# A scatter-add of graph messages: more groups sent as pairs, one product for a pair, leftovers of 112 rows, kept groups one at a time

## The chip, the cores and the metric

One core of a Trainium2 chip. The metric is the device time of one execution in microseconds; the kernel before takes 3864.85 us, the median of three runs (3861.75 to 3872.72). A core has engines with instruction streams of their own: TensorE (PE; its weight loads are shown as PEld), VectorE (DVE), ScalarE (ACT), GpSimd (POOL) and SyncE (SP, which here issues transfers). They wait for each other, and for transfers, on semaphores.

## The reference

A graph layer: 12500 nodes with 128 features, 400000 edges with 20 edge features. Edges are sorted by `dst`; `src` is random. Cut to what matters:

```
h   = relu(layernorm(x)) @ W_in2f.T
Wij = (smu(edge_attr @ W_f1.T + b_f1) @ W_f2.T + b_f2) * edge_weight[:, None]
x_ij = h[dst] * Wij                                  # one 128-float message per edge
agg = segment_sum(x_ij, src, num_segments=12500)     # added up by src
out = x + smu(agg @ W_o1.T + b_o1) @ W_o2.T + b_o2
```

Gathering `h[dst]` is easy, since `dst` is sorted and a run of edges touches a window of few nodes. Adding up by `src` is not: the messages must first be brought into the order of `src`.

## The kernel before, in words

**Tiles, groups, epochs.** The edges are cut into 3125 tiles of 128, groups of 4 tiles (`GRP`) and supergroups of 8 (`SUP`, two groups): 391 supergroups, 782 groups. The nodes are cut into 98 bins of 128. The supergroups are cut into ten epochs (`PARTS`); each epoch has a buffer in HBM with `CAP` rows for each bin, and three such buffers are used in turn. `CAP` follows from the mean number of rows in a bin, `SIGMA` deviations and the share of pairs, rounded up to 128 rows.

**Making messages.** In each step of the main loop the engines work on a few neighbouring groups at different stages: PE `hide`, ACT `bend` (the gelu), PE `gather` (one-hot times the window of h), ACT `take` (scaled by the weight, L945), PE `weigh` (L970, L972), DVE `mix` (the product, L1002), which writes the message tile `ms`: four tiles of 128 features and, in column 128, the node's place within its bin. There are nine message tiles; one is free again when its scatter has landed.

**Where a row goes.** DVE marks each edge's bin (`bins`), PE counts ranks within bins (`count`, L735), DVE reads them (`read`, L779) and makes row numbers `ix` (`number`). POOL then scatters the message rows into the epoch's buffer, one indirect transfer of 128 rows for each tile (L1072).

**Pairs.** In a paired group tiles 0 and 1 are matched with tiles 2 and 3: an edge of the first half is put beside an edge of the second half that has the same bin and rank, and both go as one row of double width. The keys of the first half are spread over a PSUM bank by PE (`spread_keys`, L813), DVE compares them (`match`, L822, which counts the matches in `met`), PE ranks the unmatched rows (`rank_left`, L832) and DVE makes a permutation of them (`place_left`, L839, L840). A step later PE permutes the second half by 12 passes (`permute`, L859), ACT takes the result out of PSUM (`take_pairs`, L870, L871), and POOL sends two transfers of 128 double rows. The unmatched rows, the leftover `lt`, are sent with a later group, its host, which also counts them (`el`, L707). A pair takes two scatters and one for its leftover, a plain group four. In the kernel before, the product of a pair is made in two halves: tiles 0 and 1 into `ms` (L992), tiles 2 and 3 into a tile `cd` of two buffers (L991), with a copy of the places for each (L995 or L997). From epoch 1 on, and after group 80 of epoch 0, about every third group is a pair.

**Kept groups.** The 23 supergroups of the last two epochs are made early, spread over epochs 1 to 4 (the list `flow`), both groups in a row. Their message rows are written to HBM (`kept_rows`), not scattered; at the end, in the late loop, they are fetched again (`refill`) and scattered while the sums of the last epochs run. A kept group passes the PSUM bank `pt` on its way (`turn`, L1027), and ACT copies it out (L1040). Nine of them are paired in the late loop.

**Summing.** While epoch k is scattered, the buffer of epoch k-1 is fetched (`rw`), DVE makes one-hot matrices of the places (`choose`, L1117) and PE adds the rows up into `agg` (L1130, 4116 products in all, of two passes each). The number of products follows from `CAP` alone.

**Order.** PE, DVE, ACT and SP run their instructions in the order in which the code gives them; the main loop writes that order out by hand, step by step. Work that is not tied to a step, such as reading later edge indices (`head_of`), stands in a timetable, with slots that the loop passes three times a step: `fetched` issues the transfers of `dst_col` and `src_col`, and `based` (L410) is DVE's first use of them. `double` (L644) is an ACT copy of the bins that DVE's `mark_bins` (L654) reads.

**The guard.** If a bin overflows, or a pair matches too few rows, a flag is set and the kernel computes everything again in a slow, general way.

Of the kernel before, what the change touches and what calls it, by code (L numbers as in the profile page):

```python
# [20 lines left out]
P = 128  # L21
# [11 lines left out]
PARTS = (60, 58, 58, 58, 47, 37, 27, 23, 16, 7)  # L33
EVERY = (4, 3, 3, 3, 3, 3, 3, 3)
UNPAIRED = 10
MOST_PAIRS = 224
FIRST_PAIRED = 80
LATE_EVERY = 3
# [3 lines left out]
SIGMA = 4.95  # L42
# [8 lines left out]
def gnn_kernel(  # L51
# [46 lines left out]
    for a, n in eps_of:  # L98
        last_groups = UNPAIRED / (SUP // GRP)
        paired = n - last_groups if 0 < len(CAP) < len(eps_of) - 1 else 0  # L100
        if not CAP:
            paired = max(0, n - last_groups - FIRST_PAIRED / (SUP // GRP))
        every = LATE_EVERY if len(CAP) >= len(eps_of) - SENT_LAST else EVERY[len(CAP)]
        mean = (n + WIDER * paired / every) * SUP * P * P / N
        dev = SIGMA * math.sqrt((n + 2 * WIDER * paired / every) * SUP * P * P / N)
        CAP.append(math.ceil((mean + dev) / P) * P)
        ZMIN.append(max(0, math.floor((n * SUP * P * P / N - dev) / ZP) * ZP) if len(ZMIN) < BUFS else 0)
# [14 lines left out]
    SPILLS = 2  # L122
# [222 lines left out]
    with tc.tile_pool(name="ld", bufs=4) as ld, \  # L345
# [121 lines left out]
        met = const.tile([P, 2 * MOST_PAIRS], F16, name="met")  # L467
        h_first = met.bitcast(BF)[:, :3 * D].rearrange("p (b k d) -> p b k d", b=1, k=3)
# [57 lines left out]
        seq = [s * PER + i for s in flow for i in range(PER) if s * PER + i < NG]  # L526

# [11 lines left out]
        for p, g in enumerate(seq):  # L539
# [3 lines left out]
            if wanting and p >= wanting[0][0] + 5:  # L543
                host[g] = wanting.pop(0)[1]
                assert epoch[g // PER] == epoch[host[g] // PER]
            elif (since_pair >= (math.floor, math.ceil)[len(paired) % 2](EVERY[epoch[g // PER]])
                  and (epoch[g // PER] or p >= FIRST_PAIRED) and seq[p - 1] // PER < EARLY and g + UNPAIRED < ends_of[epoch[g // PER]]):
                paired[g] = len(paired)
                wanting.append((p, g))
                since_pair = 0  # L550
        assert not wanting
        LATE_END = eps_of[-1][0] * PER - 1
        late_pairs = list(range(EARLY * PER + LATE_EVERY - 1, LATE_END - 3, LATE_EVERY))
        pair_no = {g: i for i, g in enumerate(list(paired) + late_pairs)}
        assert 2 * len(pair_no) <= met.shape[1]
        late_keys = const.tile([P, len(late_pairs), GRP], F32, name="late_keys")
# [91 lines left out]
        def mark_bins(s):  # L648
# [3 lines left out]
            es = cnt.tile([P, SUP // 2, NB], F16, name="es", bufs=1)  # L652
# [129 lines left out]
        def number(g):  # L782
# [4 lines left out]
            if s_of(g) < EARLY:  # L787
                ix = cnt.tile([P, GRP + 1], I32, name="ix", bufs=12)
# [18 lines left out]
        keys_of, left_of, matched, apart_of = {}, {}, {}, {}  # L807

        def spread_keys(g):

            kt = ps1.tile([P, GRP * P], F32, name="pt")
# [4 lines left out]
        def match(g):  # L816
# [3 lines left out]
            o = 2 * pair_no[g]  # L820
            for i in range(2):
# [3 lines left out]
                                               op0=ALU.is_equal, op1=ALU.mult, accum_out=met[:, o + i:o + i + 1])  # L825
            matched[g] = (kt, pp)

        def rank_left(g):

            kt, i = matched[g][0], 2 * pair_no[g]  # L830
            at_ = kt[:, 2 * P:2 * P + 2]
            nc.tensor.matmul(at_, tri, met[:, i:i + 2], start=True, stop=False, skip_group_check=True)  # L832
            nc.tensor.matmul(at_[:, 1:2], ones_h, met[:, i:i + 1], start=False, stop=True, skip_group_check=True)
# [17 lines left out]
        def permute(g):  # L851

            pp, cd = matched.pop(g)[1], apart_of.pop(g)
            po = ps1.tile([P, GRP * P], F32, name="pt")
            for j in range(3):
                w = ROW + 1 if j == 2 else ROW
                for i in range(2):
                    o = (4 + i if j == 2 else 2 * i + j) * P
                    nc.tensor.matmul(po[:, j * (ROW + 1):j * (ROW + 1) + w], pp[:, o:o + P], cd[:, i, :w],  # L859
                                     start=(i == 0), stop=(i == 1))  # L860
            matched[g] = po

        def take_pairs(g):

            po, ms, k = matched.pop(g), mixed[g], epoch[s_of(g)]
            lt = cnt.tile([P, ROW + 1], F32, name="lt", bufs=3)
# [3 lines left out]
            nc.scalar.activation(ms[:, 1::2, :], po[:, :o].rearrange("p (j r) -> p j r", j=2)[:, :, 0:ROW], AF.Copy)  # L870
# [105 lines left out]

        def mix(g):
# [3 lines left out]
            if by_edge(g):  # L981
                t, n = groups[g]
                ms = msg.tile([P, GRP, ROW], F32, name="ms")
                pw, hg = pws.pop(g), rows_of.pop(g)
                if g in paired:
                    k = epoch[s_of(g)]
                    m, t0, hic = k // BUFS, *begins[k]
                    cd = msg.tile([P, 2, ROW + 1], F32, name="cd", bufs=2)
                    pw, hg = [v.rearrange("p (j f) -> p j f", f=P) for v in (pw, hg)]
                    nc.scalar.activation(taken[g][:, :2], keys_of[g][:, :2], AF.Copy)  # L990
                    nc.vector.tensor_tensor(cd[:, :, 0:P], pw[:, 2:], hg[:, 2:], op=ALU.mult)  # L991
                    nc.vector.tensor_tensor(ms[:, 0::2, 0:P], pw[:, :2], hg[:, :2], op=ALU.mult)  # L992
                    for to, a in ((cd, t + 2), (ms[:, 0::2], t)):
                        if m:
                            nc.scalar.activation(to[:, :, P], lo_b[:, a:a + 2], AF.Identity, bias=mark[:, m:m + 1])  # L995
                        else:
                            nc.scalar.activation(to[:, :, P], lo_b[:, a:a + 2], AF.Copy)  # L997
                    nc.scalar.activation(cd[:, :, P + 1], hic[:, t + 2 - t0:t + 4 - t0], AF.Identity, bias=shift)
                    apart_of[g] = cd
                    mixed[g] = ms  # L1000
                    return
                nc.vector.tensor_tensor(ms[:, :n, 0:P], pw.rearrange("p (j f) -> p j f", f=P)[:, :n],  # L1002
# [27 lines left out]
        def send(g):  # L1030
# [5 lines left out]
            ms = msg.tile([P, GRP, ROW], F32, name="ms")  # L1036
# [17 lines left out]
        def scatter(g, ms):  # L1054

            ix = taken.pop(g)
            if g in pair_no:
                for j in range(2):
                    scatter_rows(g, ms[:, 2 * j:2 * j + 2].rearrange("p j r -> p (j r)"), ix[:, j:j + 1])
# [3 lines left out]
            if g in host:  # L1063
                scatter_rows(g, left_of.pop(host[g])[0], ix[:, GRP:])
# [168 lines left out]
        ms = msg.tile([P, GRP, ROW], F32, name="ms")  # L1233
# [205 lines left out]
        for c in range(1, NC):  # L1439
# [3 lines left out]
            due(t + 0.5 - (SOONER if t < known else 0), stages.pop(0))  # L1443
# [193 lines left out]
        for p in range(len(seq)):  # L1637
# [80 lines left out]
            if p % PER == 0:  # L1718
                double(sup_at(p // PER + 2), nc.scalar)
# [39 lines left out]
        def refill(g):  # L1759
            if g < NG:  # L1760
                t, n = groups[g]
                back[g] = msg.tile([P, GRP, ROW], F32, name="ms")
                if g in pair_no:
                    t0, hic = begins[epoch[s_of(g)]]
                    cd = apart_of[g] = msg.tile([P, 2, ROW + 1], F32, name="cd", bufs=2)
                    nc.sync.dma_start(back[g][:, 0::2, :], kept_rows[:, t - kept_tile:t - kept_tile + 2, :])
                    nc.sync.dma_start(cd[:, :, 0:ROW], kept_rows[:, t - kept_tile + 2:t - kept_tile + 4, :])
                    nc.scalar.activation(cd[:, :, P + 1], hic[:, t + 2 - t0:t + 4 - t0], AF.Identity, bias=shift)
                    mixed[g] = back[g]
                    return  # L1770
                nc.sync.dma_start(back[g][:, :n, :], kept_rows[:, t - kept_tile:t - kept_tile + n, :])

        def flag_formed():

            few_met = ps1.tile([P, GRP * P], F32, name="pc")[:, :2 * len(pair_no)]
            nc.tensor.matmul(few_met, ones_h, met[:, :2 * len(pair_no)], start=True, stop=True)
            sums = mv.rearrange("p b s -> p (b s)")[:, :len(pair_no)]
            nc.vector.tensor_reduce(sums, few_met.rearrange("p (g i) -> p g i", i=2), op=ALU.add, axis=AX.X)
            least_met = const.tile([P, 1], F32, name="least_met")
            nc.vector.tensor_reduce(least_met, sums, op=ALU.min, axis=AX.X)  # L1780
            i = 4 + 2 * EPOCHS
            nc.vector.tensor_scalar(bad[:, i:i + 1], least_met, float(P), None, op0=ALU.is_lt)
# [27 lines left out]
        def place_of_left(g):  # L1810
# [4 lines left out]
            ix = ranks[g] = cnt.tile([P, GRP + 1], I32, name="ix", bufs=12)  # L1815
# [258 lines left out]
```

## Time and profile before

| | |
|---|---|
| median of three runs | 3864.85 us |
| the profiled execution | 3877.55 us, span 3875.5 us |
| PE / DVE / ACT / POOL busy | 85% / 79% / 73% / 75% |
| indirect transfers on POOL | 2578 + 192 + 163 |
| bytes moved | 904.79 MB, 233 GB/s on average |

How to read it: the page has each engine's busy time, the span in 40 slices, the transfer queues, the chain that ended last, and groups of instructions by line. A row of a group has the line, engine, operation, what it writes and reads, the count, busy us in all and mean ns of one; then the idle time of the engine before these, and what ended it. L12 is line 12 of the kernel. An indirect transfer's length on POOL is the time in which POOL makes its descriptors, not that of its data. An engine's idle time is put down to the event that came last before it went on, which need not be what it waited for.

### The profile page before, as it was taken

What the parts mean: (1) busy time and instruction counts of PE and PEld (TensorE: products, weight loads), DVE (VectorE), ACT (ScalarE), POOL (GpSimd) and SP (SyncE); (2) the same over time, 40 slices, a digit from 0 to 9 for tenths busy, and PEclk for the clock granted to TensorE, in tenths of its full rate; (3) what the DMA queues carried; (4) which work ended last, traced back from release to release, by engine and by line L of the source; (5) the groups of instructions that cost most, each with busy time, mean ns of one, the idle gap of its engine ahead of it and who ended that gap; (6) DMA issues with size and microseconds to landing.
All of it is one profiled execution on the core that took longest, in us unless ns stands there. A gap on an engine that the chain in (4) does not pass through costs nothing.

```text
span 3875.5 us, 89505 instructions
## 1 busy us (share of the span) xinstructions
PE 3289.4 (85%) x27505; PEld 2851.7 (74%) x27505; DVE 3066.3 (79%) x8171; ACT 2831.6 (73%) x8043; POOL 2889.8 (75%) x2977
## 2 busy tenths in 40 slices
PE   8766677888888888899888889899989988999667
PEld 4345555777777777788777778788888878888557
DVE  7887786778777888888888888888888877888557
ACT  7776666778777888788888888788877876776102
POOL 6777777777677777777777777777777777777776
PEclk9988898999999999999999999999999999999889
DMA  5887878889897877788887878878888888887988
GB/s 155 225 238 222 235 222 236 243 242 257 249 264 222 230 220 222 225 238 230 227 225 221 239 213 249 235 230 234 246 234 237 245 233 226 237 237 213 285 258 241
DMA packets 663934, 904.79 MB, mean 233 GB/s; under 512 B 180372, under 2 KB 463128, under 8 KB 663322
## 3 DMA queue, kind: packets, MB, share of 16 engines
q1 hardware_dynamic: 556025, 666.99, 63.4%
q0 software_dynamic: 100112, 219.73, 17.6%
q10 hardware_dynamic: 7312, 12.29, 0.9%
q8 instruction: 223, 3.65, 0.4%
q14 instruction: 262, 2.14, 0.2%
HBM read 500.66 MB, written 398.03 MB: 232 GB/s over the span
## 4 chain that ended last, share of the span: by engine, by line
PE 31%; DVE 17%; DMA 17%; issue 8%; ACT 8%; POOL 7%; SPq 1%; DVEq 0%; ACTq 0%; POOLq 0%
DMA buf<-ms,ix 11%; PE pg L1130 10%; POOL buf L1072 7%; PE pw L970 6%; PE pt L859 5%; PE pc L735 3%; ACT hg L945 3%; DVE se L1117 3%; DVE pc L779 2%; DMA rbc<-rel_dram 2%; DVE mt L822 2%; DVE ms L1002 2%; PE ph L926 2%; DVE eo L654 2%; DMA buf<-lt,ix 2%
## 5 line engine op out<-in xcount | busy, mean ns | idle before, releaser
L1072 POOL DMA_INDIRECT buf<-ms,ix x2578 | 2506.5, 972 | 846.6 <-issue 566.1
L1130 PE MATMUL pg<-se,rw 128*128 128x128 f32 x8036 | 1171.4, 285 | 116.6 <-DVE se L1117 52.7
L1130 PEld LDWEIGHTS pg<-se,rw 128*128 128x128 f32 x8036 | 1042.0, 195 | 162.6 <-DVE agg L1144 56.6
L945 ACT ACTIVATE hg<-ph,w_sb 128x128 f32<-128x128 f32 x2784 | 788.6, 364 | 491.3 <-PE ph L926 468.0
L970 PE MATMUL pw<-w_f,ge 128*128 128x128 f32 x5568 | 778.3, 284 | 12.7 <-DVE ms L1002 7.6
L970 PEld LDWEIGHTS pw<-w_f,ge 128*128 128x128 f32 x5568 | 701.1, 197 | 31.1 <-ACT ge L898 8.0
L1117 DVE TENSOR_TENSOR se<-irow_ps,rw 128x1536 f32<-128x1536 f32 (+1 forms) x345 | 587.4, 1703 | 94.3 <-DMA rw<-buf 74.6
L779 DVE TENSOR_REDUCE pc<-pc 128x4 f32<-128x392 f32 (+1 forms) x782 | 463.6, 593 | 154.5 <-PE pc L735 150.4
L617 ACT ACTIVATE oh<-rbc,nrow 128x512 bf16<-128x512 uint8 x724 | 538.2, 743 | 38.9 <-DMA rbc<-rel_dram 38.9
L618 ACT ACTIVATE oh<-oh,onesb 128x512 bf16<-128x512 bf16 x742 | 535.3, 721 | 24.2
L1002 DVE TENSOR_TENSOR ms<-pw,hg 128x512 f32<-128x512 f32 x513 | 351.4, 685 | 128.5 <-PE pw L972 42.6
L859 PE MATMUL pt<-cd,mt 128*128 128x129 f32 (+1 forms) x2304 | 311.2, 287 | 82.4 <-DVE at L839 76.1
L735 PE MATMUL pc<-eo,tri 128*128 128x392 f16 x782 | 266.9, 341 | 110.2 <-DVE ix L801 88.4
L859 PEld LDWEIGHTS pt<-cd,mt 128*128 128x128 f32 x2304 | 286.5, 199 | 96.5 <-issue 49.6
L926 PE MATMUL ph<-hw,oh 126*128 126x128 bf16 x2784 | 280.7, 224 | 24.0 <-ACT hg L945 24.0
L898 ACT ACTIVATE ge<-pu 128x512 f32<-128x512 f32 x452 | 275.6, 610 | 18.7 <-PE pu L890 16.7
L735 PE MATMUL pc<-so,ones_h 128*128 128x392 f16 (+1 forms) x965 | 281.4, 314 | 0.0
L972 PE MATMUL pw<-wls,f 128*128 128x128 bf16 x2784 | 273.7, 222 | 0.0
L735 PEld LDWEIGHTS <-ones_h 128*128 128x128 f16 x1554 | 154.9, 100 | 149.1 <-issue 32.7
L926 PEld LDWEIGHTS <-oh 126*128 126x128 bf16 x2784 | 220.0, 100 | 45.6 <-issue 28.1
L654 DVE TENSOR_TENSOR eo<-irow_ps,ed 128x784 f16<-128x784 f16 x391 | 218.2, 558 | 37.2 <-ACT ed L644 34.2
L1072 POOL DMA_INDIRECT buf<-lt,ix x192 | 185.9, 968 | 65.5 <-issue 28.7
(339 smaller groups left out, 5088.7 us busy)
## 6 DMA issues: line engine op xcount, KB each, us to landing
rw<-buf SPq DMA_DIRECT2D x292, 774.0 KB
f<-f_parts SPq DMA_DIRECT2D x370, 240.0 KB
buf<-zero SPq DMA_DIRECT2D x146, 387.0 KB
rbc<-rel_dram SPq DMA_DIRECT2D x389, 128.0 KB
buf<-ms,ix POOLq DMA_INDIRECT x2578
f_parts<-hs SPq DMA_DIRECT2D x104, 360.0 KB
rw<-buf SPq DMA_DIRECT2D x49, 645.0 KB
f_parts<-hs SPq DMA_DIRECT2D x106, 240.0 KB
```

The costliest lines, as they stand in the source:

```text
L617: nc.scalar.activation(oh, loaded[s][1][:, o:o + n], AF.Abs, bias=pneg if s < FEW // SUP else nrow)
L618: nc.scalar.activation(oh, oh, AF.Relu, scale=-1.0, bias=onesb[:, 0:1])
L735: nc.tensor.matmul(to, by, of, start=start, stop=stop, skip_group_check=True)
L779: nc.vector.tensor_reduce(sl[:, :n], pc[:, :n], op=ALU.max, axis=AX.X)
L859: nc.tensor.matmul(po[:, j * (ROW + 1):j * (ROW + 1) + w], pp[:, o:o + P], cd[:, i, :w], start=(i == 0), stop=(i == 1))
L926: nc.tensor.matmul(ph[:, j * P:(j + 1) * P], oh[:3 * WIN, a:a + P], hw[:3 * WIN, g % PER, :], start=True, stop=True)
L945: nc.scalar.activation(hg[:, j * P:(j + 1) * P], rows_of[g][:, j * P:(j + 1) * P], AF.Copy, scale=w_sb[:, t + j:t + j + 1])
L970: nc.tensor.matmul(pw[:, a:a + P], ge[:, a:a + P], w_f2, start=(a == 0), stop=False, skip_group_check=True)
L1002: nc.vector.tensor_tensor(ms[:, :n, 0:P], pw.rearrange("p (j f) -> p j f", f=P)[:, :n], hg.rearrange("p (j f) -> p j f", f=P)[:, :n], op=A ...
L1072: i = nc.gpsimd.indirect_dma_start(out=(wide if g in host or g in pair_no else bufs)[k][:, :], out_offset=bass.IndirectOffsetOnAxis(ap=ix, ...
L1117: nc.vector.tensor_tensor(se[:, a:a + n], own.unsqueeze(1).to_broadcast([P, n, P]), rows_in[c][:, a:a + n, P:P + 1].to_broadcast([P, n, P] ...
L1130: nc.tensor.matmul(pgs[0][:, g, :], rows_in[c][:, o, 0:P], sel[c][:, o, :], start=(q == 0), stop=(q == Q[k] - 1))
```

## The change

- `PARTS`: one supergroup goes from epoch 0 to epoch 7. `SIGMA` 4.95 becomes 4.6.
- Pairs: every 3 groups in epoch 0 from group 50 on (before: 4, from 80), and at 2 and 3 groups in turn in epochs 1 to 7 (before: 3). A group is a pair ahead of being a host, and not within two places behind a kept group (before: one).
- A pair's product is one instruction, into a message tile seen as two halves of 2 x 129 + 1 columns; `permute` reads its second half from there, and `take_pairs` writes the permuted rows back over it. `cd` is gone.
- Leftovers are sent with 112 rows, and the guard's bound is raised to 144 matches. A leftover has six tiles (before: three); in the late loop it lies in free tiles of another kind.
- Kept groups alternate with sent ones.
- `double` is called one step earlier for later supergroups; every head's `fetched` is due nine slots earlier, not only the first heads'; `es` has two buffers, `ix` ten (before: twelve).
- Late loop: five groups are fetched ahead (before: four), the keys are spread in the bank `pw`, and `place_of_left` comes ahead of `number_left`.
- Some constants move into space that is free by then (`late_keys` into `mv`, further match counts into `down`).

```diff
-PARTS = (60, 58, 58, 58, 47, 37, 27, 23, 16, 7)
-EVERY = (4, 3, 3, 3, 3, 3, 3, 3)
+PARTS = (59, 58, 58, 58, 47, 37, 27, 24, 16, 7)
+EVERY = (3,) + (2.5,) * 7
-FIRST_PAIRED = 80
-LATE_EVERY = 3
+FIRST_PAIRED = 50
+LATE_OF = 1, 3
+LATE_FREE = 6
+LEFT_ROWS = 112
-SIGMA = 4.95
+SIGMA = 4.6
...
+        for p in reversed(range(len(seq) - 1)):
+            a, b = seq[p:p + 2]
+            if a // PER >= EARLY and a % PER and b // PER < EARLY:
+                seq[p], seq[p + 1] = b, a
...
-            if wanting and p >= wanting[0][0] + 5:
-                host[g] = wanting.pop(0)[1]
-            elif (since_pair >= (math.floor, math.ceil)[len(paired) % 2](EVERY[epoch[g // PER]])
-                  and (epoch[g // PER] or p >= FIRST_PAIRED) and seq[p - 1] // PER < EARLY and g + UNPAIRED < ends_of[epoch[g // PER]]):
+            k = epoch[g // PER]
+            if (since_pair >= (math.floor, math.ceil)[len(paired) % 2](EVERY[k]) and (k or p >= FIRST_PAIRED)
+                    and max(seq[p - 2:p]) // PER < EARLY and g + UNPAIRED < ends_of[k]):
                 paired[g] = len(paired)
                 wanting.append((p, g))
                 since_pair = 0
+            elif wanting and p >= wanting[0][0] + 5:
+                host[g] = wanting.pop(0)[1]
...
-            es = cnt.tile([P, SUP // 2, NB], F16, name="es", bufs=1)
+            es = cnt.tile([P, SUP // 2, NB], F16, name="es", bufs=2)
...
-                ix = cnt.tile([P, GRP + 1], I32, name="ix", bufs=12)
+                ix = cnt.tile([P, GRP + 1], I32, name="ix", bufs=10)
...
-            kt = ps1.tile([P, GRP * P], F32, name="pt")
+            kt = ps1.tile([P, GRP * P], F32, name="pt" if g in paired else "pw")
...
-                    nc.tensor.matmul(po[:, j * (ROW + 1):j * (ROW + 1) + w], pp[:, o:o + P], cd[:, i, :w],
+                    nc.tensor.matmul(po[:, j * (ROW + 1):j * (ROW + 1) + w], pp[:, o:o + P], ms[:, i, ROW:ROW + w],
...
-            lt = cnt.tile([P, ROW + 1], F32, name="lt", bufs=3)
+            lt = cnt.tile([P, ROW + 1], F32, name="lt", bufs=6) if g in paired else late_left(g)
...
-            nc.scalar.activation(ms[:, 1::2, :], po[:, :o].rearrange("p (j r) -> p j r", j=2)[:, :, 0:ROW], AF.Copy)
+            nc.scalar.activation(ms[:, :, ROW:2 * ROW], po[:, :o].rearrange("p (j r) -> p j r", j=2)[:, :, 0:ROW], AF.Copy)
...
-                    nc.vector.tensor_tensor(cd[:, :, 0:P], pw[:, 2:], hg[:, 2:], op=ALU.mult)
-                    nc.vector.tensor_tensor(ms[:, 0::2, 0:P], pw[:, :2], hg[:, :2], op=ALU.mult)
-                    for to, a in ((cd, t + 2), (ms[:, 0::2], t)):
-                        if m:
-                            nc.scalar.activation(to[:, :, P], lo_b[:, a:a + 2], AF.Identity, bias=mark[:, m:m + 1])
-                        else:
-                            nc.scalar.activation(to[:, :, P], lo_b[:, a:a + 2], AF.Copy)
-                    nc.scalar.activation(cd[:, :, P + 1], hic[:, t + 2 - t0:t + 4 - t0], AF.Identity, bias=shift)
+                    nc.vector.tensor_tensor(by_tile(ms)[:, :, :, 0:P], pw, hg, op=ALU.mult)
+                    place = lo_b[:, t:t + GRP].rearrange("p (a u) -> p a u", a=2)
+                    if m:
+                        nc.scalar.activation(by_tile(ms)[:, :, :, P], place, AF.Identity, bias=mark[:, m:m + 1])
+                    else:
+                        nc.scalar.activation(by_tile(ms)[:, :, :, P], place, AF.Copy)
+                    nc.scalar.activation(ms[:, :, 2 * ROW], hic[:, t + 2 - t0:t + 4 - t0], AF.Identity, bias=shift)
...
-                scatter_rows(g, left_of.pop(host[g])[0], ix[:, GRP:])
+                scatter_rows(g, left_of.pop(host[g])[0][:LEFT_ROWS], ix[:LEFT_ROWS, GRP:])
...
-            due(t + 0.5 - (SOONER if t < known else 0), stages.pop(0))
+            due(t + 0.5 - SOONER, stages.pop(0))
...
-            if p % PER == 0:
-                double(sup_at(p // PER + 2), nc.scalar)
+            if p == 0 or p % PER:
+                double(sup_at(-(-p // PER) + 2), nc.scalar)
...
-        for g in range(g1, g1 + 4):
+        AHEAD_OF = 5
+        for g in range(g1, g1 + AHEAD_OF):
             refill(g)
```

The helper that gives the pair's product its view of the tile:

```python
def as_pairs(ms):
    return ms.rearrange("p (u r) -> p u r", u=2)

def by_tile(pairs):
    return pairs[:, :, 0:2 * ROW].rearrange("p u (a r) -> p a u r", a=2)
```

106 lines of the change are left out of this document (63 added, 43 removed).

## The prediction

> **What bounds the kernel now.** I read the page first (busy shares), then GpSimd's own rows, then the span cut into its stages, then the sums of waits.
>
> ```profile
> span 3875.5 us, 89505 instructions
> PE 3289.4 (85%) x27505; PEld 2851.7 (74%) x27505; DVE 3066.3 (79%) x8171; ACT 2831.6 (73%) x8043; POOL 2889.8 (75%) x2977
> ```
>
> By busy time PE is the fullest engine and POOL is one of three at about three quarters. That reading misleads for POOL. Its rows by line, and its own timeline (start, length, idle before it):
>
> ```profile
> L1072 POOL DMA_INDIRECT buf<-ms,ix x2578 | 2506.5, 972 | 846.6 <-issue 566.1 <-DMA buf<-ms,ix 40.5 <-ACT hg L945 27.8
> L1072 POOL DMA_INDIRECT buf<-lt,ix x192 | 185.9, 968 | 65.5 <-issue 28.7 <-DVE ix L804 7.9 <-DVE pc L779 3.7
> L1072 POOL DMA_INDIRECT buf<-ms,ix_kept x163 | 156.7, 962 | 49.7 <-issue 46.0 <-DMA buf<-ms,ix_kept 1.8 <-DMA hic<-in_x 0.3
> ```
>
> ```profile
> 1205.90 0.96 POOL L1072 DMA_INDIRECT buf<-ms,ix  x1 [0.30 <-DMA buf<-ms,ix]
> 1207.16 0.96 POOL L1072 DMA_INDIRECT buf<-ms,ix  x1 [0.30 <-DVE ix L801]
> 1208.43 0.96 POOL L1072 DMA_INDIRECT buf<-ms,ix  x1 [0.30 <-issue]
> ```
>
> Each scatter is preceded by the same 0.30 us, whoever is named as its releaser: the name is chance, the gap is part of the price. So one scatter costs 0.97 + 0.30 = 1.27 us of POOL, and 2578 + 192 + 163 = 2933 of them take 3725 of the 3875 us. The 192 leftovers also count the pairs. By stage (busy of each engine, number of its instructions, granted clock):
>
> ```profile
> core 0: us, PE busy (x) PEld busy (x) DVE busy (x) ACT busy (x) POOL busy (x), PEclk, DMA share, GB/s
> 250.00:700.00 450.00, 312.61 (x2475) 257.05 (x2475) 333.39 (x986) 305.90 (x899) 338.29 (x345) 0.86 0.81 229
> 700.00:1700.00 1000.00, 874.18 (x7554) 771.53 (x7552) 784.10 (x2142) 806.20 (x2356) 736.68 (x758) 0.96 0.83 237
> 1700.00:2700.00 1000.00, 901.30 (x7948) 802.45 (x7949) 831.22 (x2232) 836.86 (x2372) 753.96 (x779) 0.98 0.81 231
> 2700.00:3570.00 870.00, 798.50 (x7141) 729.01 (x7140) 733.76 (x1879) 663.74 (x1877) 662.13 (x682) 0.97 0.84 235
> 3570.00:3820.00 250.00, 168.26 (x1278) 150.48 (x1277) 144.68 (x230) 21.02 (x50) 187.38 (x195) 0.87 0.83 262
> ```
>
> Some of POOL's waits in 700–1700 (us in total, times, longest), then the first of 2700–3570:
>
> ```profile
> POOL buf L1072 <- issue: 175.3, 546, 2.9
> POOL buf L1072 <- ACT hg L945: 14.1, 19, 8.0
> ...
> POOL buf L1072 <- issue: 148.5, 487, 0.3
> ```
>
> Where the longest is 0.3, every wait is the constant gap, 148.5 / 487 = 0.305 us; only the earlier stage has real ones. POOL's busy time plus 0.305 us for each of its instructions is its floor in a stage: 443 of 450, 968 of 1000, 992 of 1000, 870 of 870, 247 of 250. POOL is nearly full everywhere, with 7, 32, 8, 0 and 3 us over. PE, which makes the messages together with DVE and ACT, is at 87, 90 and 92% in the three long stages. What ties the two sides is a message buffer that has not landed. The sums of waits over the whole span say how often that happened, and which other waits the change touches:
>
> ```profile
> DVE base_i L410 <- DMA rw<-in_dst_col: 37.9, 3, 15.0
> DVE eo L654 <- ACT ed L644: 34.2, 36, 4.3
> PE pt L813 <- ACT ms L1040: 24.1, 8, 6.3
> DVE ms L1002 <- DMA buf<-ms,ix: 21.1, 21, 2.5
> ACT lt L871 <- DMA buf<-lt,ix: 17.7, 11, 5.6
> ACT ms L1052 <- DMA buf<-ms,ix: 10.3, 6, 6.2
> ```
>
> The producers stood still for want of a buffer for only 21.1 + 17.7 + 10.3 = 49 us. So they would not run much faster if scatters were free: the kernel has two limits, POOL and the producers' loop, within about 2% of each other. Fewer scatters alone cannot pay in full; what the edit does to the producers decides with them.
>
> **The change, part by part.** Walking the loop that chooses pairs with the old and the new constants gives 183 and 214 early pairs, and 9 late ones in both (183 + 9 is the 192 above). A pair replaces four scatters by two and a leftover, so 31 pairs remove 31 scatters: 2933 become 2902, 31 x 1.27 = **39 us of POOL**. By place in the old order, pairs go from 14 to 27 in 250–700, 61 to 64, 59 to 64, and 49 to 59 in the three long stages. The capacities CAP stay 768 (four times), 640, 512, 384, 384, 256, 128, so the summing matmuls, fetches and clears do not change: lower SIGMA and higher pair share cancel.
>
> Leftovers of 112 rows instead of 128: no row has another row count for this operation. The nearest are POOL's two plain DMAs, of 128 and of 84 rows:
>
> ```profile
> L218 POOL DMA_DIRECT2D buf<-zero x1 | 0.8, 763 | 0.0
> L489 POOL DMA_DIRECT2D h_dram<-zero x1 | 0.6, 577 | 0.0
> ```
>
> That is 186 ns for 44 rows, 4.2 ns a row, so 16 rows are 0.068 us and 223 leftovers 15 us. The bounds are 0 (all fixed) and 16/128 of 0.968 us, 27 us. A loss is excluded, since no row is added. I take 15, as it is the only row that varies the count. The Trainium skill (DMA: Bandwidth & Descriptors, Anatomy of one DMA — SWDGE (gpsimd) path) calls descriptor generation small and says many descriptors can be emitted before their cost shows; by that the term is 0 and the sum below some 10 us later.
>
> What a pair costs the producers:
>
> ```profile
> L859 PE MATMUL pt<-cd,mt 128*128 128x129 f32 x1536 | 219.7, 288 | 82.4 <-DVE at L839 76.1 <-ACT ms L1050 3.2 <-ACT oh L618 1.4
> L813 PE MATMUL pt<-ident,key 128*128 128x128 f32 x366 | 76.0, 291 | 107.6 <-DVE key L795 79.5 <-ACT ms L1040 24.1 <-ACT oh L617 2.6
> L832 PE MATMUL pt<-met,tri 128*128 128x2 f16 x192 | 32.1, 167 | 22.7 <-DVE mt L822 21.5
> L735 PE MATMUL pc<-el,tri 128*128 128x98 f16 x183 | 38.0, 208 | 0.0
> L822 DVE SCALAR_TENSOR_TENSOR mt<-pt,key,onesb 128x256 f32<-128x256 f32 x366 | 161.7, 479 | 21.1 <-PE pt L813 19.9
> L840 DVE TENSOR_TENSOR mt<-irow_ps,at 128x256 f32<-128x256 f32 x192 | 81.5, 424 | 6.6
> L707 DVE TENSOR_SCALAR el<-mv,lat 128x98 f16<-128x98 f32 x183 | 53.8, 294 | 0.3
> L870 ACT ACTIVATE ms<-pt 128x258 f32<-128x258 f32 x192 | 78.9, 411 | 75.4 <-PE pt L859 75.4
> L992 DVE TENSOR_TENSOR ms<-pw,hg 128x256 f32<-128x256 f32 x183 | 76.0, 415 | 2.5 <-issue 2.4
> L1002 DVE TENSOR_TENSOR ms<-pw,hg 128x512 f32<-128x512 f32 x513 | 351.4, 685 | 128.5 <-PE pw L972 42.6 <-DMA buf<-ms,ix 21.1 <-ACT hg L945 20.9
> L995 ACT ACTIVATE ms<-lo_b,mark 128x2 f32<-128x2 uint8 x108 | 30.5, 282 | 2.4 <-issue 2.3
> ```
>
> PE: 8 of the 12 permuting passes of a pair take 219.7 / 192 = 1.14 us, so 12 take 1.7; the two key transposes 0.4; two ranks 0.3; the host's two counts of 208 ns, with overlap, 0.3: **2.7 us of PE a pair**. DVE: 0.96 + 0.42 + 0.29 and four small ones, about 2.5 us. ACT: 0.41 and three smaller, 1.2 us. For 31 pairs that is 84 us of PE, 78 of DVE, 37 of ACT.
>
> One product for a pair gives back DVE 2 x 0.415 - 0.685 = 0.145 us and ACT one of two lo_b copies, 0.28 (less in early epochs), on all 214: 31 us of DVE, some 50 of ACT. So ACT ends with less work than before, DVE with 47 us more, PE with the full 84. Bounds for the new product: it writes a four-way strided view that no row shows; I take the 0.685 of the same 512 columns, and 0.83 (no gain) as the other end.
>
> The rest removes waits. Every later head's fetch is issued nine slots earlier, which moves it ahead of the base copy: the 38 us of DVE standing for in_dst_col (all three waits lie in 250–700; the heads that already had the nine slots show none); nothing, if POOL's backlog covered them. Kept groups no longer stand in twos, and no pair follows within two places of one: the 24 us of PE behind the kept group's copies (L813 <- L1040; in 700–1700 alone the first row below), and POOL's idle 32 us there, which is where a kept couple sends nothing for two steps. The doubled bins move half a step earlier: up to 34 us of DVE behind ed, taken at half, since the engine's next input is often late too, and spread evenly over four stages. Six leftover tiles for three: ACT's 17.7, all in 2700–3570. ix 12 to 10 costs nothing while the nine message tiles, taken in the same step, run out first; if it did bind, it would show as a wait of L801, at most one scatter group, 5 us, each time. AHEAD_OF, the second key bank and the earlier place_of_left act in 3570–3820, where POOL is full, with the same 9 late pairs: only their shorter leftovers count, 1 us. Two rows of the waits in 700–1700, where all of L1052's 10.3 us lie too:
>
> ```profile
> PE pt L813 <- ACT ms L1040: 17.1, 4, 6.3
> ...
> DVE ms L1002 <- DMA buf<-ms,ix: 9.9, 10, 1.3
> ```
>
> A rule against the change: the Trainium skill (SBUF — State Buffer, Who interferes with whom) says a DVE tensor_scalar in a two-port mode locks GpSimd out of writing descriptors. The pairs bring 31 more el; if each blocked POOL for its whole length, that is 31 x 0.29 = 9 us, and the sum would be 3824. The rows bear out little: scatters average 972 ns against the 0.96 us of the timeline's, over every kind of DVE work.
>
> **The sum, by stage** (the larger of POOL's new floor and the producers' new time, plus what the two lose against each other):
> - 250–700: floor 443 - 13 x 1.27 - 27 x 0.068 = 425. Producers 450 - 38 + 13 pairs x 2.7 at half (PE is at 69% here) = 430. Takes 430: -20.
> - 700–1700: floor 968 - 4 - 4 = 960. Producers 1000 - 20 (buffers) - 17 (L813) - 4 (ed) + 3 x 2.7 = 967. With half of POOL's 32 idle us left: 976: -24.
> - 1700–2700: floor 992 - 6 - 4 = 982. Producers 1000 - 11 (the other L1002 waits) - 7 - 4 + 13 = 991; 992: -8.
> - 2700–3570: floor 870 - 13 - 4 = 853. Producers 870 - 18 (lt) - 4 + 27 - 4 (product, half of 59 x 0.145) = 871; 873: +3. Here PE, at 92%, eats what POOL saves.
> - Late: -1.
>
> Together -50. The profiled execution took 3877.55 us (span 3875.5), 0.3% over the median of 3864.85; I put the -50 on the median: **3815 us**.
>
> **The rivals.**
> (a) POOL's floor is reached everywhere: the producers have more slack than their waits show, because an engine slowed by a full queue does not always show a wait for a buffer. For it: the longest POOL wait of 0.3 us after 2700. Against: only 49 us of buffer waits in all. Time: 3865 - 39 - 15 - 47 (idle in 250–2700) = 3764.
> (b) PE's loop becomes the bound, slower: in 700–3570, 18 more pairs x 2.7 = 49 us of PE. If PE can't be filled beyond its present 90% there ((874 + 901 + 799) / 2870), these take 54 us, and waits taken away elsewhere only turn into others, like the 76.1 us of PE behind DVE's at. Less the 20 of 250–700: 3899. It decides as soon as POOL in 2700–3570 shows idle gaps over 0.3 us while PE stays at 92%.
> (c) The two cancel, within 0.3%: the 39 us are given back after 2700 and the waits removed were covered by POOL's backlog: about 3860.
> (d) The guard trips and the slow path runs: at least two POOL transfers for each of 3125 tiles, 7.9 ms more. Counting the inputs, a pair leaves 63 to 106 rows (112 allowed), and no bin passes 722 of 768.
>
> **How the numbers follow.** Forecast 0.5 (3785 to 3850 by itself), (a) 0.18, (b) 0.16, (c) 0.15, (d) 0.01. A measurement of this kernel tells 0.3%, some 12 us, from no change, so the forecast and (a) are faster, and a little of (c): 0.69; same 0.15; slower 0.16. The range takes (a) at 3765 and much of (b) at 3885; with the row term at 0 or 27, the forecast stays inside.
>
> **What will show it.** 2902 scatters, 223 of them lt; lt's mean near 0.90 us if rows count, 0.968 if not. The in_dst_col wait gone. POOL's waits of more than 0.35 us in 700–1700 mostly gone. L1002 at 685 ns in place of L991 and L992. PE's share in 2700–3570 at 94% or more if the step there holds; if it stays at 92% with POOL idle, (b) was right and this forecast wrong; if the scatters follow each other without a gap from 250 to 3800, (a).

## The result and the profile after

The changed kernel takes 3829.82 us (median of four runs, 3826.85 to 3834.66) against 3868.72 for the kernel before, run beside it: a ratio of 0.9901, 95% interval 0.9887 to 0.9916, some 38 us faster. 3815 was predicted, in a range of 3765 to 3885. The profiled executions differ by 50.7 us (3877.55 and 3826.85), their spans by 50.4. The page's first part and GpSimd's groups by form, after:

```profile
span 3825.1 us, 90354 instructions
PE 3294.2 (86%) x28066; PEld 2872.9 (75%) x28066; DVE 3116.8 (81%) x8275; ACT 2839.2 (74%) x7986; POOL 2855.5 (75%) x2946
...
L1110 POOL DMA_INDIRECT buf<-ms,ix x2516 | 2444.3, 971 | 813.6 <-issue 569.0 <-DMA buf<-ms,ix 54.0 <-ACT ms L1090 39.9
L1110 POOL DMA_INDIRECT buf<-lt,ix x214 | 203.3, 950 | 78.0 <-issue 27.7 <-DVE ix L821 16.6 <-DVE pc L796 4.6
L1110 POOL DMA_INDIRECT buf<-ms,ix_kept x163 | 158.3, 971 | 49.7 <-issue 45.7 <-DMA buf<-ms,ix_kept 2.1 <-ACT ms L898 0.3
L1110 POOL DMA_INDIRECT buf<-ge,ix x9 | 8.8, 979 | 2.7 <-issue 1.8 <-DMA w_sb<-in_x 0.3 <-ACT ms L1806 0.3
```

There are 2516 + 214 + 163 + 9 = 2902 scatters, as walked out beforehand. The third number after the bar is the idle time ahead of the group; 0.305 us of it belongs to each scatter. What is left over is idle time that something caused; below it is called a **real gap**, summed from the single scatters of a trace. From the rows it comes out about 6 us higher in every kernel (here 944.0 - 2902 x 0.305 = 59), because the rows also hold the 8 us wait ahead of the first scatter, at 13 us.

With that, the gain can be booked on POOL. Its busy time fell from 2889.8 to 2855.5 (-34.3); 31 constant gaps are gone (-9.5); real gaps fell from 60.9 to 52.7 (-8.2); the time ahead of the first and behind the last scatter grew by 1.6. Together -50.4, the change of the span. This is bookkeeping and no cause: causes show in where the real gaps lie. Before: 6.9 us in 250–700, 20.6 from there to 1110, 20.7 in 1110–2700, none later. After: 20.5, 21.4, 1.0 and 0.7. From 1110 us on POOL hardly ever waits, but the early stages did not improve. GpSimd's first waits in 700–1200 and in 1200–2700 (us in total, times, longest):

```profile
POOL buf L1110 <- issue: 80.8, 265, 0.3
POOL buf L1110 <- ACT ms L1090: 22.7, 14, 5.1
```

```profile
POOL buf L1110 <- issue: 268.4, 880, 0.3
POOL buf L1110 <- DMA buf<-ms,ix: 25.0, 82, 0.3
```

In the first window ACT's place copy (L1090) makes POOL wait up to 5.1 us; in the second the two that lead have no wait above the constant. The same five stretches of time as in the prediction, in the profile after (busy of each engine with its number of instructions, then granted clock, DMA share, GB/s):

```profile
250.00:700.00 450.00, 336.36 (x2713) 280.26 (x2712) 356.71 (x1079) 316.45 (x930) 327.40 (x335) 0.91 0.82 233
700.00:1700.00 1000.00, 891.98 (x7930) 795.50 (x7929) 818.26 (x2186) 840.14 (x2401) 744.44 (x769) 0.98 0.86 244
1700.00:2700.00 1000.00, 915.66 (x8177) 820.32 (x8175) 851.85 (x2247) 840.94 (x2358) 759.90 (x786) 0.99 0.83 235
2700.00:3570.00 870.00, 773.51 (x7052) 710.69 (x7051) 723.72 (x1848) 623.36 (x1759) 661.20 (x684) 0.97 0.81 232
3570.00:3820.00 250.00, 191.47 (x1481) 174.67 (x1479) 168.53 (x276) 40.64 (x77) 183.81 (x182) 0.90 0.87 270
```

PE is at 89% in 2700–3570 (773.5 of 870), not at 94%. From the sums of waits over the whole span:

```profile
ACT ms L1088 <- DVE ms L1040: 219.7, 167, 4.0
ACT ms L1090 <- DVE ms L1040: 145.7, 106, 8.7
...
ACT hg L973 <- PE ph L954: 80.4, 108, 3.3
...
PE pt L875 <- DVE at L855: 48.2, 47, 2.3
...
ACT ms L1034 <- DVE ms L1031: 44.7, 60, 2.2
...
DVE ms L1040 <- DMA buf<-ms,ix: 36.5, 27, 4.7
```

DVE's wait for `in_dst_col` is gone, as is PE's for the kept group's copy. New, and not foreseen, are the first two rows and the L1034 one: ACT's copy of the places (L1088, L1090, L1034) now waits for DVE's product of the same message tile, 410 us in all. No such row stood before; there ACT waited 468.0 us for PE's `ph` instead, now 80.4:

```profile
ACT hg L945 <- PE ph L926: 468.0, 273, 19.7
```

The two write different columns (place: 128, product: 0 to 127), but the tile is now one flat row seen through rearranged views, and the wait says that the views were taken to overlap.

The product of a given group is made at these times, read from the starts of DVE's products in each trace (us; the kernels are named below):

| | group 118 | 352 | 560 | 735 | last scatter | end |
|---|---|---|---|---|---|---|
| before | 607 | 1749 | 2741 | 3566 | 3816 | 3875 |
| after | 605 | 1718 | 2691 | 3507 | 3764 | 3825 |
| pairs spaced as before | 602 | 1710 | 2695 | 3527 | 3786 | 3845 |
| places free | 598 | 1697 | 2676 | 3492 | 3751 | 3811 |
| fetches as before | 613 | 1721 | 2700 | 3517 | 3775 | 3836 |
| kept groups in twos | 608 | 1752 | 2743 | 3549 | 3805 | 3866 |
| two products | 599 | 1702 | 2682 | 3501 | 3758 | 3818 |

By the products, of the 50 us, 2 are won by group 118, 29 by 352, 19 by 560, 9 by 735, and 9 are lost behind it. But the producers' lead over POOL changes, and POOL issues last. The first scatters of five groups that stand at the bounds of the stages before (us; the `ms` scatters counted in order, four for a plain group and two for a pair):

| | group 44 | 133 | 337 | 547 | 730 | last scatter | end |
|---|---|---|---|---|---|---|---|
| before | 249 | 696 | 1696 | 2698 | 3569 | 3816 | 3875 |
| after | 247 | 687 | 1670 | 2657 | 3515 | 3764 | 3825 |

By these, 3 us are won ahead of 250, 6 in 250–700, 18, 14 and 14 in the three long stages, and 4 are lost behind them. The product of group 547 lies 7.5 us ahead of its first scatter before, and 18.5 after.

### The profile page after: what moved, and what is told of

It is laid out like the page before. It is cut to its first block, busy times and chain, and to the rows that moved or that the text cites. A ratio compares the mean times of both kernels' runs of the same rounds, so it can differ in the third digit from the quotient of the medians.

```text
span 3825.1 us, 90354 instructions
## 1 busy us (share of the span) xinstructions
PE 3294.2 (86%) x28066; PEld 2872.9 (75%) x28066; DVE 3116.8 (81%) x8275; ACT 2839.2 (74%) x7986; POOL 2855.5 (75%) x2946
## 4 chain that ended last, share of the span: by engine, by line
PE 33%; DMA 18%; DVE 16%; ACT 11%; issue 11%; POOL 9%; SPq 2%; ACTq 0%; DVEq 0%; POOLq 0%
DMA buf<-ms,ix 12%; PE pg L1168 10%; POOL buf L1110 9%; PE pw L998 6%; PE pt L875 5%; ACT hg L973 3%; PE pc L752 3%; DVE se L1155 3%; DVE mt L838 2%; DVE ms L1040 2%; ACT oh L634 2%; ACT ge L926 2%; PE ph L954 2%; PE pw L1000 1%; DVE pc L796 1%
## 5 line engine op out<-in xcount | busy, mean ns | idle before, releaser
L1110 POOL DMA_INDIRECT buf<-ms,ix x2516 | 2444.3, 971 | 813.6 <-issue 569.0
L973 ACT ACTIVATE hg<-ph,w_sb 128x128 f32<-128x128 f32 x2784 | 781.9, 361 | 94.5 <-PE ph L954 80.4
L635 ACT ACTIVATE oh<-oh,onesb 128x512 bf16<-128x512 bf16 x743 | 536.0, 721 | 24.2
L1040 DVE TENSOR_TENSOR ms<-pw,hg 128x512 f32<-128x512 f32 x482 | 330.2, 685 | 137.8 <-DMA buf<-ms,ix 36.5
L875 PE MATMUL pt<-ms,mt 128*128 128x129 f32 x2676 | 345.0, 279 | 55.0 <-DVE at L855 48.2
L875 PEld LDWEIGHTS pt<-ms,mt 128*128 128x128 f32 x2676 | 319.1, 193 | 66.7 <-issue 23.3
L1088 ACT ACTIVATE ms<-lo_b,mark 128x4 f32<-128x4 uint8 x309 | 91.3, 295 | 231.9 <-DVE ms L1040 219.7
L1110 POOL DMA_INDIRECT buf<-lt,ix x214 | 203.3, 950 | 78.0 <-issue 27.7
```

What stands on the lines that cost most here:

```text
L635: nc.scalar.activation(oh, oh, AF.Relu, scale=-1.0, bias=onesb[:, 0:1])
L973: nc.scalar.activation(hg[:, j * P:(j + 1) * P], rows_of[g][:, j * P:(j + 1) * P], AF.Copy, scale=w_sb[:, t + j:t + j + 1])
L1110: i = nc.gpsimd.indirect_dma_start(out=(wide if g in host or g in pair_no else bufs)[k][:, :], out_offset=bass.IndirectOffsetOnAxis(ap=ix, ...
```

## The experiments

Theory 1: POOL's scatters set the time wherever it has no real gaps. Theory 2: the producers' loop (PE, DVE and ACT, which make the messages) does. Each kernel is the changed one with one edit, and ratios are against the kernel before on the same chip; the changed kernel has 0.9901, so 0.001 is 3.9 us. The first four kernels ran on a chip where every kernel, the one before too, took 5.7 to 6.0 ms. In the traces from there all five engines stand still together for 406 to 438 us (31 in after), about a fifth of the extra time; what makes up the rest isn't shown. Ratios there (0.9859 with pairs spaced as before, 0.9558 with leftovers of 128 rows, 0.9634 with places free, 0.9743 with a pair at every second group) are not compared with the others, and only the length of one instruction is used. Three of the four are the same kernels as in the table.

| edit | ratio, 95% | scatters | span | POOL busy | real gaps | of them 250–700 | 700–1110 | 1110–2700 | later |
|---|---|---|---|---|---|---|---|---|---|
| none (after) | 0.9901 (0.9887–0.9916) | 2902 | 3825.1 | 2855.5 | 52.7 | 20.5 | 21.4 | 1.0 | 0.7 |
| pairs spaced as before | 0.9959 (0.9945–0.9974) | 2946 | 3845.3 | 2899.8 | 16.9 | 3.8 | 3.7 | 0.3 | 0.7 |
| leftovers not sent | 0.9770 (0.9755–0.9786) | 2688 | 3763.2 | 2667.1 | 246.7 | 42.5 | 48.5 | 92.0 | 57.0 |
| places free | 0.9878 (0.9859–0.9896) | 2902 | 3811.4 | 2859.3 | 36.4 | 9.6 | 18.9 | 1.1 | 0.2 |
| every second group | 1.0001 (0.9989–1.0013) | 2848 | – | – | – | – | – | – | – |
| places free, late pairs | 0.9869 (0.9854–0.9885) | 2888 | 3807.4 | 2845.8 | 48.8 | 11.8 | 13.0 | 0.6 | 15.9 |
| fetches as before | 0.9935 (0.9921–0.9948) | 2902 | 3835.6 | 2863.9 | 56.3 | 20.9 | 24.2 | 1.1 | 0.2 |
| kept groups in twos | 1.0007 (0.9996–1.0019) | 2884 | 3866.1 | 2841.9 | 113.2 | 22.1 | 35.8 | 48.4 | 0.2 |
| two products | 0.9915 (0.9902–0.9929) | 2902 | 3817.6 | 2867.0 | 36.1 | 11.3 | 17.6 | 0.3 | 0.2 |

The columns do for every row what was done above: busy time, 0.305 us for each scatter and real gaps carry the differences of the spans within 3 us (what the stages lack of the real gaps lies ahead of 250 us). For the kept groups in twos, against after: -13.6 - 5.5 + 60.5 = 41.4, span +41.0.

### Pairs spaced as before

```diff
-EVERY = (3,) + (2.5,) * 7
+EVERY = (4,) + (3,) * 7
-FIRST_PAIRED = 50
+FIRST_PAIRED = 80
```

> The changed kernel with the old share of pairs, all else as changed, once more, because on the first chip every kernel, the one before too, took about 5.9 ms. 2933 scatters. Theory 1, POOL's row of scatters sets the time: about 39 us slower than the changed kernel, level with the kernel before. Theory 2, the producers' loop sets it: within 10 us of the changed kernel, so some 30 us faster than the kernel before.

Its groups on GpSimd, and its first waits in 700–1200:

```profile
L1110 POOL DMA_INDIRECT buf<-ms,ix x2604 | 2529.3, 971 | 817.6 <-issue 597.4 <-DMA buf<-ms,ix 60.2 <-ACT ge L926 22.6
L1110 POOL DMA_INDIRECT buf<-lt,ix x170 | 162.1, 953 | 51.8 <-issue 24.4 <-DVE pc L796 4.0 <-DVE so L718 3.1
```

```profile
POOL buf L1110 <- issue: 90.6, 291, 2.1
POOL buf L1110 <- DMA buf<-ms,ix: 9.1, 30, 0.3
POOL buf L1110 <- ACT ms L1090: 4.3, 8, 2.1
```

Under the new rules of placing, the old spacing gives 44 pairs fewer than after, not 31. These 44 scatters are 44 x 1.27 = 56 us of POOL, and the time differs by 0.0058, 22 us, between the two theories. The rest is in the gaps: 36 us fewer. With fewer pairs POOL hardly ever waits, so it alone sets the time; with more pairs the producers fall behind it until 1110 us and give back over half.

Against before, this kernel has 13 pairs fewer and 13 scatters more, and still is 0.0041, 16 us, faster: its real gaps are 16.9 us in place of 60.9. So of the 38 us, 22 came with the pairs and 16 with the rest of the change; this edit doesn't tell how the parts of that rest share them.

### Leftovers not sent

The early leftovers (214 scatters) are not sent; the output lacks their rows, and nothing else is left out: the pairs, permutations and leftover tiles are still made, and the host's count compares with other numbers of the same form.

```diff
-                scatter_rows(g, left_of.pop(host[g])[0][:LEFT_ROWS], ix[:LEFT_ROWS, GRP:])
+                left_of.pop(host[g])
...
-                    nc.vector.tensor_scalar(lot, bin_row, left_of[host[g]][1], None, op0=ALU.is_equal)
+                    nc.vector.tensor_scalar(lot, bin_row, drow[:, 0:1], None, op0=ALU.is_equal)
```

> The changed kernel with the 214 early leftovers neither given a place nor sent (their edges are missing from the sums); everything that the other engines do stays, POOL has 2688 scatters. It shows the producers' own time. Theory 1 with slack in the producers: 214 x 1.24 = 265 us less POOL work, so 60 us or more faster than the changed kernel, up to where PE binds. Theory 2, the two limits within 2%: at most 50 us faster, with PE at 92% or a little more in the long stages and POOL with real gaps everywhere.

Two of its stages, and GpSimd's first waits in 1200–2700:

```profile
1700.00:2700.00 1000.00, 913.34 (x8195) 826.88 (x8303) 863.66 (x2279) 853.71 (x2396) 719.62 (x738) 1.00 0.82 234
2700.00:3570.00 870.00, 787.90 (x7092) 726.03 (x7175) 740.71 (x1851) 608.48 (x1710) 619.78 (x635) 0.98 0.84 244
```

```profile
POOL buf L1110 <- issue: 260.1, 852, 0.6
POOL buf L1110 <- ACT ms L1088: 68.2, 48, 3.5
POOL buf L1110 <- ACT ms L1090: 42.5, 31, 3.1
```

268 us of POOL's work bring 0.0131, 51 us (by the spans, 62): the producers then set the time, POOL waits in every stage, and PE stands at 91% in both rows, no more than in 1700–2700 of after (92%). So the producers' own time lies 51 us, 1.3%, under the changed kernel, or a little more, since DVE still waits 25 us for message buffers here: two limits that close, as predicted.

### Places free

The place copies are declared independent of the product of their tile.

```diff
-                nc.vector.tensor_tensor(ms[:, :n, 0:P], ...)
-                places_in(g, ms)
+                pr = nc.vector.tensor_tensor(ms[:, :n, 0:P], ...)
+                tc.add_to_no_dep_group("products", pr.ins)
+                tc.declare_no_dep(places_in(g, ms).ins, group="products", reason="other columns")
```

> The changed kernel in which ACT's copy of the places does not wait for DVE's product of the same tile, once more on another chip. If the wait only moved ACT's idle time: within 5 us of the changed kernel. If it holds the producers back before 1110 us, where POOL has 41 us of gaps: 10 to 30 us faster, those gaps halved. If the producers set the time everywhere: 30 us faster or more.

From its sums of waits on ACT:

```profile
ACT hg L973 <- PE ph L954: 340.7, 246, 6.4
```

ACT waits for PE again, as before the change, so the wait did hang on the order that was taken to be needed. Its price is not shown. The ratio is 0.0023 lower, 9 us, where 10 to 30 were expected, and the two intervals overlap. Real gaps in 250–700 halve and group 118 is made 7 us earlier; but the kernel with two products, further below, keeps the wait and has nearly the same in its trace, 11.3 us of gaps there and group 118 at 599:

```profile
ACT ms L1089 <- DVE ms L1041: 206.0, 156, 5.4
```

So 9 us is an estimate. For it speaks that the two kernels without the wait have the two lowest ratios of those that compute everything.

### A pair at every second group

```diff
-EVERY = (3,) + (2.5,) * 7
+EVERY = (3,) + (2,) * 7
-SIGMA = 4.6
+SIGMA = 4.2
```

> The changed kernel with a pair at every second group in epochs 1 to 7 and SIGMA 4.2 (CAP the same), once more on another chip: 277 pairs, 2848 scatters, 54 fewer. Theory 1: 60 to 68 us faster than the changed kernel, no POOL gaps after 1110 us. Theory 2: 54 x 2.7 = 146 us more of PE at 92%: slower by 30 us or more. Between: real POOL gaps after 1110 us and a gain under 40 us.

With 54 pairs more POOL has 54 x 1.27 = 69 us less to do, and the time is 0.0100, 39 us, longer, as Theory 2 had it. Where it waits is not shown, since the only trace is of an execution of 11,035 us and isn't used; that POOL's scatters don't set this time is.

### Places free, and more pairs only where POOL has no gaps

```diff
-EVERY = (3,) + (2.5,) * 7
+EVERY = (3,) + (2.5,) * 4 + (2,) * 3
-SIGMA = 4.6
+SIGMA = 4.4
```

> Edit: the copy of the places no longer waits for the product of the same message tile, and pairs stand at every second group only from the fifth stretch of the graph on (237 pairs and 2888 scatters instead of 223 and 2902). Theory 1 (POOL's scatters set the time wherever POOL has no gaps, from about 1110 us on, and the producers have room left there): the 14 scatters fewer give 14 x 1.25 = 17 us against the kernel whose place copies are free (3812.6 us with before at 3859), so about 3796 us, ratio about 0.983. Theory 2 (the producers' loop is already the longer one late): 14 pairs more cost 14 x 1.65 = 23 us, so about 3835 us, ratio about 0.994. Between them a ratio of 0.986 to 0.988 means that the two limits have met.

GpSimd's waits in 2700–3570, where after has no wait above 0.8:

```profile
POOL buf L1112 <- issue: 143.6, 469, 0.8
POOL buf L1112 <- DVE ix L821: 15.5, 10, 3.2
```

Against the kernel with free places, 14 scatters fewer save 14 x 1.27 = 18 us of POOL, and 15.9 us of real gaps appear just there. The time is 0.0009 lower, within what can be measured: the two limits have met at 237 pairs. It has the lowest ratio of all kernels that compute everything.

### Fetches as before

```diff
-            due(t + 0.5 - SOONER, stages.pop(0))
+            due(t + 0.5 - (SOONER if t < known else 0), stages.pop(0))
```

> Edit: the stages that bring the later heads of the weights are again due where they were before the change, not earlier. The prediction's step for 250 to 700 us: the wait of about 38 us for the late column comes back and with it 20 to 38 us of the time, so 3850 to 3868 us, ratio 0.995 to 1.000. Theory 1 (POOL had a backlog in that stretch, and the late column cost nothing that ended later): at most 5 us, ratio 0.990 to 0.9915.

```profile
DVE base_i L414 <- DMA rw<-in_dst_col: 8.2, 2, 6.1
```

Only 8.2 of the 37.9 us of that wait come back: so most of it did not hang on the nine slots alone; what else in the change took it away isn't shown. Group 118 is 8 us later, the end 0.0034, 13 us. That lies between the two theories; of the 10.5 us by which the spans differ, 8.4 are POOL's busy time with the same scatters (974 ns in place of 971), which the edit doesn't explain, and 3.6 are gaps, less 1.5 behind the last scatter. So 4 to 13 us, not 20 to 38.

### Kept groups in twos

```diff
-        for p in reversed(range(len(seq) - 1)):
-            a, b = seq[p:p + 2]
-            if a // PER >= EARLY and a % PER and b // PER < EARLY:
-                seq[p], seq[p + 1] = b, a
```

> Edit: the kept groups are again made two in a row, not one at a time between sent groups (the planner then makes 9 pairs more: 2893 scatters or a few fewer). The prediction's step for 700 to 1700 us: POOL's idle time of 33 us at the kept groups comes back, 24 us of it in the end, less about 11 us for the nine scatters fewer, so about +13 us, ratio about 0.9935; POOL's gaps beyond the constant 0.305 us rise from 52 us to about 75 us. Theory 1 (POOL is late by the producers anyway until 1110 us): the order moves the gaps and not the end, ratio 0.987 to 0.990.

GpSimd's first waits in 1200–2700, and its timeline where a kept couple is made (DVE's kept products start at 1322.5 and 1326.9):

```profile
POOL buf L1106 <- issue: 255.2, 830, 2.4
POOL buf L1106 <- ACT ms L1084: 21.8, 31, 2.4
POOL buf L1106 <- DMA buf<-ms,ix: 20.7, 68, 0.3
POOL buf L1106 <- DVE ix L817: 19.8, 17, 2.2
```

```profile
1326.10 0.95 POOL L1106 DMA_INDIRECT buf<-ms,ix  x1 [1.15 <-ACT lt L895]
1327.36 0.96 POOL L1106 DMA_INDIRECT buf<-ms,ix  x1 [0.30 <-issue]
1329.69 0.93 POOL L1106 DMA_INDIRECT buf<-lt,ix  x1 [1.38 <-DVE ix L817]
1332.51 0.97 POOL L1106 DMA_INDIRECT buf<-ms,ix  x1 [1.89 <-ACT ms L1086]
```

The planner makes 18 pairs more here, not nine. Even so the kernel is 0.0106, 41 us, slower than after, where 13 were expected, and no faster than before: the rest of the change, with these 18 pairs, brings nothing in this order. Of 84 us of real gaps in 700–2700, 53 lie within 10 us behind the start of a kept product; after has 22, of which less than 1 lies there. That fits a couple that leaves POOL without new messages for two steps, with a queue too short to cover them. The 18 pairs are part of the edit, so how the 41 us divide between them and the order isn't settled.

### The product of a pair as two instructions

```diff
-                    nc.vector.tensor_tensor(by_tile(ms)[:, :, :, 0:P], pw, hg, op=ALU.mult)
+                    for a in range(2):
+                        nc.vector.tensor_tensor(by_tile(ms)[:, a, :, 0:P], pw[:, a], hg[:, a], op=ALU.mult)
```

> Edit: the product of a pair is made by two instructions of 128x256 again instead of one of 128x512. It adds about 0.145 us of the vector engine to each of 214 pairs, 31 us in all. Theory 1 (POOL's scatters set the time from 1110 us on): only the third of the pairs before 1110 us can cost, at most 8 us, so 3830 to 3838 us beside before at 3868, ratio 0.990 to 0.992. Theory 2 (the producers' loop sets the time): most of the 31 us come back, 15 to 31 us, ratio 0.994 to 0.998.

The pair's product, first after, then here:

```profile
L1031 DVE TENSOR_TENSOR ms<-pw,hg 128x512 f32<-128x512 f32 x214 | 146.7, 685 | 57.9 <-ACT hg L973 20.2 <-PE pw L1000 16.5 <-DMA buf<-ms,ix 8.6
```

```profile
L1032 DVE TENSOR_TENSOR ms<-pw,hg 128x256 f32<-128x256 f32 x428 | 161.2, 415 | 57.7 <-PE pw L1000 14.2 <-DMA buf<-ms,ix 13.2 <-ACT hg L973 9.1
```

Two halves take 0.83 us, one whole 0.685, as taken beforehand. The 31 us of DVE move the time by 0.0014, no difference that these intervals can tell: Theory 1.

### Leftovers of 128 rows

```diff
-LEFT_ROWS = 112
+LEFT_ROWS = 128
```

> The changed kernel with leftovers of 128 rows. By the lengths in the two traces (lt median 0.932 us at 112 rows, 0.958 at 128) 223 x 0.026 us = 6 us slower if POOL sets the time; by the prediction's 0.068 us a leftover, 15 us slower; if the producers set it, no difference.

The leftover's scatters here and after, each from the view of the tile `lt` (ns: shortest, median, longest):

```profile
L1110 POOL DMA_INDIRECT buf<-lt,ix x214: 952/957/1137, 378.3 to 5329.5; - x107
```

```profile
L1110 POOL DMA_INDIRECT buf<-lt,ix x214: 927/932/1412, 305.2 to 3503.6; - x107
```

Sixteen rows fewer take 25 ns off, 1.6 ns a row; 223 leftovers make 6 us. This compares single instructions; the edit's effect on the time wasn't measured where it could be told.

## Why the prediction was right, and where not

**Two limits within 2%: right.** The kernel with no early leftovers puts the producers 1.3% under the changed one, and the pair counts show the crossing: 44 pairs fewer cost 22 us, 54 more cost 39 us, and with free places 14 more late ones change nothing. That is why rival (a), POOL's floor everywhere, did not come: 41.9 us of real gaps remain in 250–1110. Rival (c), both cancel, falls with the ratio's interval, which ends at 0.9916. Rival (b) did not come either: its sign (real gaps after 2700 with PE at 92%) appears only in the kernel with 237 pairs, at 798.83 busy us of 870:

```profile
2700.00:3570.00 870.00, 798.83 (x7303) 733.95 (x7302) 746.34 (x1963) 620.77 (x1787) 649.61 (x672) 0.99 0.82 237
```

**The sum came out by parts that cancel, which is luck.** By stage, -20, -24, -8, +3 and -1 were predicted, and -6, -18, -14, -14 and +4 came, with -3 ahead of 250 (from the table of first scatters). That the -50 meets the two traces is luck once more: the medians lie 38.9 us apart, and the profiled execution of before is 5 us slower than the slowest of the four timed beside after.

- **250–700, a step that failed:** -20 for -6. It counted the 38 us that DVE stood for `in_dst_col` as won. The wait is gone, and POOL has 11 scatters fewer between groups 44 and 133, 14 us; but its real gaps there grew from 6.9 to 16.9 us. With the fetches undone alone, 8.2 us of the wait come back and group 118 is 8 us later. The gaps came with the denser pairs (3.8 us in 250–700 with pairs spaced as before, 20.5 in after); whether ACT's new wait has a share isn't settled.
- **700–1700: right in kind, too large**, -24 for -18. POOL's idle time around the kept couples was real: before, 27.4 of its 32.6 us of gaps lie within 30 us behind the start of a kept product, a stretch that covers 40% of the time. It was taken at half; between groups 133 and 337 the real gaps went from 32.6 to 25.2, and what is left lies ahead of 1110. What the alternation is worth by itself isn't shown, since the kernel in twos has more pairs too.
- **1700–2700: undersized**, -8 for -14: 5 scatters fewer are 6 us, and the gaps went from 8.7 to 0.9. The step had the producers at 991; from the product of group 337 to that of 547 they took 981, and POOL 987.
- **2700–3570, the other step that failed:** +3 for -14. "PE at 92% eats what POOL saves" did not happen: PE is at 89%, and POOL has no real gap to speak of, neither before nor after, so 10 scatters fewer pay in full, 13 us. Behind it 2 us are lost in the late loop and 2 after the last scatter, for which no run shows a reason.

**Terms of the sum.** Scatters: 31 x 1.27, as predicted. Rows: 15 us taken, 6 measured, because a plain transfer's 4.2 ns a row isn't the price in a scatter (1.6). The Trainium skill (DMA: Bandwidth & Descriptors, Anatomy of one DMA — SWDGE (gpsimd) path), by which descriptors cost little until there are many, was nearer than that row. Product: 685 ns, as taken. Waits: DVE's for `ed` fell from 34.2 to 9.7 us, and ACT's 17.7 for a leftover tile is gone, much as counted on; what that is worth in time was not tested. A pair's passes on PE, 12 for each of 223 pairs: 345.0 / 223 = 1.55 us, where 1.7 was taken:

```profile
L875 PE MATMUL pt<-ms,mt 128*128 128x129 f32 x2676 | 345.0, 279 | 55.0 <-DVE at L855 48.2
```

**The lock of GpSimd by DVE** that the Trainium skill has (SBUF — State Buffer, Who interferes with whom), by which the sum would be 3824, isn't seen. The 189 `ms` scatters of after in whose time an `el` runs take 971 ns on average, and so do the other 2327; whether these `el` run in such a mode no run shows. **Missed altogether:** ACT's wait for the product, 410 us of waits and perhaps 9 us of time. The diff shows the new views; what they make of the order of two writes was not asked.

## What to carry to other kernels

Where two limits lie close, book the time on the engine that issues last, with its constant gap taken out, and read from the places of its real gaps which limit holds in which stage. Take a stage's gain from that engine's instructions too, since the lead of the others over it changes. Add work for the other engines only in stages without gaps. When a tile's shape or view changes, look at what else writes that tile: writes to separate columns can begin to wait for each other. A wait in the trace is not the price of its cause: of the 38 us that stood for one column, 8 came back when the fetches alone were put back, and only 13 us of time with them.

## What the runs showed of the hardware

A scatter's price on GpSimd hardly changes between 128 rows (957 ns) and 112 (932), beside a constant 0.305 us ahead of each. Scatters that do the same work can differ by 3 ns in the mean from one execution to the next (971 and 974), 8 us over the kernel, which is a good part of what 0.3% amounts to.
